# Moving loads to ScalarE's queue and making later weights earlier in a four-layer graph kernel

## The chip, the cores and the metric

The kernel runs on one core of a Trainium2 chip, in fp32. Time is the device time of one execution in microseconds (us). The executions of one kernel in one group differ by 0.2 to 0.8% from lowest to highest, so I give medians with the lowest and highest run. Verdicts use ratios: the mean time of one kernel's fast runs over the mean of the other's fast runs of the same rounds, so a ratio is not quite the quotient of the medians that I quote.

## The reference, cut to what matters

Four graph layers are applied in sequence to x of shape (8, 2048, 64), with one normalised 2048 x 2048 adjacency. Each begins with a layernorm and a relu and adds its result to x. Only layer 0 and the weights of the later layers matter here:

```python
# layer 0, in words: h = relu(layernorm(x)); T0 = h, T1 = A h, T2 = 2 A T1 - T0
# weights of a node n: sum over d of embedding[n, d] * weight[d, k]   (d = 16, k = 3)
# x += sum over k of T_k[n] @ W[n, k] + bias[n]
# layer 1: three steps, adjacency and an MLP with W1, W2, b1, b2
# layer 2: linear aggregation with w_nl, b_nl, then w_out, b_out
# layer 3: attention over the neighbours
```

## The kernel before

The eight batches are worked on as four pairs, p = 0 to 3, and the 2048 nodes as four blocks of 512, nb = 0 to 3. A product with the adjacency uses a high and a low half (H, L) of each operand. For pairs 2 and 3, T1 is made in layer 0 too (`term1`, the "first product"); the loop below then makes T2 (the "second product") and the node weights, block by block.

```python
    def load_h(p, nb, name, pool):            # h of one block, 256 KB, from memory
        t = pool.tile([P, 4, 2 * C], F32, tag="hb", name=f"hb_{name}", bufs=2)
        nc.sync.dma_start(t, hs[p][:, part(nb), :])
        return t

    def halves(src, name, pool=None):
        ...
        copies.append(nc.scalar.copy(Hq, src))                                        # "H" in traces
        nc.vector.tensor_tensor(Lq, src, Hq.bitcast(F32), op=ALU.subtract)   # "L" in traces
        return Hq, Lq

    def make_weights():
        ...                                   # small columns
        raw, tr, pr = (block("z", f"wz{i}", 3) for i in range(3))   # three tiles in all; norms use them too
        nc.gpsimd.memset(raw, 0.0)
        for i, w in enumerate((w1[:, :C], w1[:, C:], w2, w_out)):
            for hf in range(2):
                hs_ = slice(hf * C, (hf + 1) * C)
                nc.sync.dma_start(raw[hs_, i, hs_], w)
        nc.vector.tensor_copy(tr, transposed(lambda t: raw[:, t, :], "wT"))   # pt_wT on TensorE
        ...
        for i, (lhsT, rhs) in enumerate(pairs):
            nc.tensor.matmul(ps[:, i, :], lhsT, rhs, start=True, stop=True)   # wP
        nc.vector.tensor_copy(pr, ps)
        ...                                   # wb1s, rows of b_out and b2, scaling; then three stores to wD

    def node_weights(p, nb, terms, between=None):
        ...
                        nc.tensor.matmul(y[:, bb, :], terms[k][hs_, ts],
                            wt[hs_, k, dg * 512:(dg + 1) * 512], ...)         # y
        ...
                    last = nc.vector.scalar_tensor_tensor(                    # y pieces, "acc" and "odd"
                        xj, yd, ec, old, op0=ALU.mult, op1=ALU.add)

    for p in range(NP):
        def prepare(q):                       # halves of block q of the next pair
            if p == 0:
                src = l0q.tile([P, 512], F32, tag="hb", name=f"t1b_{nm}", bufs=2)
                nc.sync.dma_start(src, t1D[:, q * 512:(q + 1) * 512])
                hl_next.append(back(src, 1, q))
            elif p + 1 < NP:
                hl_next.append(halves(load_h(p + 1, q, nm, l0q), nm))
        ...
        for nb in range(NB):
            if p == NP - 1 and nb == 1:
                with tc.issue_after(chain[-1].ins):
                    make_weights()
            t2T = product(hl1, nb, nm, term(2, f"t2T_{nm}"), crow, ...)       # bv_0b to bv_3b
            ...
            t0T_next = feat_0(...)            # load_h, four transposes (pt), copy on ScalarE
            node_weights(p, nb, (t0T, t1T[nb], t2T), ...)
            t0T = t0T_next
            if nb in (1, 2):
                prepare(nb - 1)
```

Names in traces: bv_0a to bv_3a are the first product, bv_0b to bv_3b the second, pt the transposes of h, hb and hb_f loads of h, t1b loads of the second pair's T1, wz the three tiles of the weights. A program that builds the kernel puts the instructions of each engine in order; the source alone does not fix it.

## Time and profile before

| Quantity of the kernel before | value |
|---|---|
| median of 3 runs | 1300.35 us (1299.11 to 1302.89) |
| the unit of pair 3's block 1 (559.50 to 601.89 us) | 42.39 us |
| the unit after it | 28.90 us |
| half-clock stretch in the first of them | 13.65 us |
| gaps of TensorE over 1.3 us between 100 and 500 us, summed | 13.9 us |

The table is read so: TensorE sets the time, so a microsecond is won only where its stream has a gap or runs slowly. One unit has a slow stretch that its neighbour lacks; the gaps are elsewhere. A gap here is the time from the start of one matmul to the start of the next; the usual one is 0.23 us in a product and 0.43 us in a pair of y matmuls.

### The profile page before, as it was taken

How to read it: one execution, taken by the hardware profiler on the slowest of the kernel's cores; microseconds unless marked ns; L12 is line 12 of the kernel's file. 1: busy time of each engine (PE TensorE's matmuls, PEld its weight loads, DVE VectorE, ACT ScalarE, POOL GpSimd, SP SyncE). 2: the span in 40 equal slices, each digit the busy share in tenths (PEclk: the TensorE clock that was granted, in tenths of full speed). 3: DMA queues.
4: the chain of work that ended last, by engine and by line, in shares of the span. 5: the costliest groups of instructions: out<-in, count | busy, mean ns of one | idle time of the engine just before them, and what ended most of it. 6: DMA issues, size and time to landing. Idle time of an engine off the chain costs nothing.

```text
span 1295.8 us, 15644 instructions
## 1 busy us (share of the span) xinstructions
PE 1230.5 (95%) x5702; PEld 865.2 (67%) x5702; DVE 750.2 (58%) x1937; ACT 188.6 (15%) x313; POOL 224.6 (17%) x228
## 2 busy tenths in 40 slices
PE   3799999899999999999999999999999999989994
PEld 2476555455585556655558887878878878878883
DVE  5325887777747775357764435535644544566664
ACT  4541001000010000000011121112111211111110
POOL 4210111111121111011101024004201400332222
PEclk8799999999999999989999999999999999999997
DMA  9793334322343322123237535443653463433322
GB/s 252 227 240 114 86 94 111 93 73 63 95 104 82 81 78 68 35 55 86 58 83 174 107 90 158 115 93 106 159 118 90 139 130 94 151 102 106 97 67 52
DMA packets 149882, 140.11 MB, mean 108 GB/s; under 512 B 99892, under 2 KB 101940, under 8 KB 149796
## 3 DMA queue, kind: packets, MB, share of 16 engines
q1 hardware_dynamic: 137780, 106.54, 32.1%
q0 software_dynamic: 9904, 31.96, 8.7%
q8 instruction: 47, 0.77, 0.3%
q10 hardware_dynamic: 2112, 0.52, 0.2%
q14 instruction: 39, 0.32, 0.1%
HBM read 94.87 MB, written 35.73 MB: 101 GB/s over the span
## 4 chain that ended last, share of the span: by engine, by line
PE 77%; DMA 6%; DVE 6%; issue 6%; POOL 2%; ACT 1%; SPq 1%; ACTq 0%; POOLq 0%; DVEq 0%
PE bv L217 33%; PE y L580 22%; PE bn L523 4%; PE ph L742 3%; DMA st<-in_adj_dram 2%; PE bv_2b L217 2%; PE bv_3b L217 2%; DMA hb<-hs 2%; POOL rstd L169 1%; PE bv_1b L217 1%; PE bv_0a L217 1%; PE bn_u L523 1%; PE pt L229 1%; PE bv_0b L217 1%; DVE acc L589 1%
## 5 line engine op out<-in xcount | busy, mean ns | idle before, releaser
L217 PE MATMUL bv<-BT,H 128*128 128x512 f32 x1024 | 426.7, 417 | 0.0
L217 PE MATMUL bv<-BT,L 128*128 128x512 f32 x1024 | 401.3, 392 | 0.0
L217 PEld LDWEIGHTS bv<-BT,H 128*128 128x128 f32 x1024 | 192.9, 188 | 47.9 <-issue 11.5
L217 PEld LDWEIGHTS bv<-BT,L 128*128 128x128 f32 x1024 | 193.0, 188 | 47.5 <-issue 11.5
L589 DVE SCALAR_TENSOR_TENSOR acc<-y,emb,acc 128x128 f32<-128x128 f32 x512 | 176.3, 344 | 69.2 <-PE y L580 68.4
L580 PE MATMUL y<-wt,t0T 64*128 64x512 f32 x512 | 145.7, 611 | 9.2 <-DVE odd L589 9.2
L589 DVE SCALAR_TENSOR_TENSOR odd<-y,emb,odd 128x128 f32<-128x128 f32 x448 | 153.5, 343 | 0.0
L169 POOL TENSOR_TENSOR rstd<-var,mhalf 128x8 f32<-128x8 f32 x64 | 106.1, 1660 | 197.1 <-DVE var L167 191.6
L209 DVE TENSOR_TENSOR g<-bv,crow 128x512 f32<-128x512 f32 x48 | 33.2, 692 | 182.4 <-PE bv L217 182.4
L163 ACT ACTIVATE sq<-z 128x512 f32<-128x512 f32 x64 | 40.4, 631 | 404.9 <-DVE z L159 392.8
L580 PEld LDWEIGHTS y<-wt,t0T 64*128 64x128 f32 x512 | 46.8, 186 | 72.3 <-issue 66.5
L560 POOL TENSOR_TENSOR acc<-acc,wl 128x512 f32<-128x512 f32 x16 | 21.0, 1314 | 295.2 <-DVE z L159 294.0
L561 POOL DMA_DIRECT2D xs<-acc x32 | 18.0, 562 | 284.3 <-DVE acc L597 233.7
L580 PE MATMUL y<-wt,t1T 64*128 64x512 f32 x256 | 67.0, 589 | 0.0
L172 DVE SCALAR_TENSOR_TENSOR z<-z,rstd 128x512 f32<-128x512 f32 x64 | 44.7, 703 | 35.5 <-POOL rstd L169 35.5
L523 PEld LDWEIGHTS bn<-wl,g 128*128 128x128 f32 x384 | 49.4, 191 | 6.3 <-ACT g L747 3.1
L166 DVE TENSOR_REDUCE var<-sq 128x8 f32<-128x512 f32 x64 | 43.5, 680 | 16.1 <-ACT sq L163 16.1
L523 PE MATMUL bn<-wl,g 128*128 128x128 f32 x384 | 51.2, 276 | 0.7 <-ACT H L204 0.4
L689 DVE SCALAR_TENSOR_TENSOR junk<-mt,cols,st 128x512 uint8<-128x512 bf16 x64 | 49.2, 769 | 0.8 <-DMA mt<-MD 0.3
L580 PEld LDWEIGHTS y<-wt,t1T 64*128 64x128 f32 x256 | 27.6, 187 | 27.4 <-issue 27.1
L747 ACT ACTIVATE g<-g,b1s 128x512 f32<-128x512 f32 x32 | 23.2, 724 | 139.3 <-DVE g L746 139.3
L159 DVE TENSOR_TENSOR z<-acc,mean 128x512 f32<-128x512 f32 x56 | 38.3, 691 | 6.6 <-DMA hs<-z 5.0
(208 smaller groups left out, 1694.2 us busy)
## 6 DMA issues: line engine op xcount, KB each, us to landing
st<-in_adj_dram SPq DMA_DIRECT2D x128, 256.0 KB, 4.1
crow<-crowD SPq DMA_DIRECT2D x64, 256.0 KB, 3.3
hs<-z POOLq DMA_DIRECT2D x48, 256.0 KB, 2.9
hb<-hs SPq DMA_DIRECT2D x40, 256.0 KB, 3.3
xs<-acc POOLq DMA_DIRECT2D x32, 256.0 KB, 2.4
MD<-BT POOLq DMA_DIRECT2D x16, 512.0 KB, 5.1
acc<-xs SPq DMA_DIRECT2D x32, 256.0 KB, 3.5
acc<-in_x_dram SPq DMA_DIRECT2D x48, 128.0 KB, 3.7
```

Source lines behind the costliest of these rows:

```text
L159: nc.vector.tensor_tensor(g, groups(xt), mean[:, :, None].to_broadcast([P, 8, C]), op=ALU.subtract)
L163: nc.scalar.activation(sq, z, AF.Square)
L166: nc.vector.tensor_reduce(var, groups(sq), axis=AX.X, op=ALU.add)
L169: powers.append(nc.gpsimd.tensor_tensor(rstd, var, mhalf, op=ALU.pow))
L172: nc.vector.scalar_tensor_tensor(groups(h), g, 0.0, rstd[:, :, None].to_broadcast([P, 8, C]), op0=ALU.max, op1=ALU.mult)
L209: ahead.append(nc.vector.tensor_tensor(out, ps, crow, op=ALU.mult))
L217: nc.tensor.matmul(ps, hl[m // 4][i][:, m % 4, :], BT[:, m, nb * 512:(nb + 1) * 512], start=(m == 0 and i == 0), stop=(m == NCH - 1 and i ...
L523: nc.tensor.matmul(ps[:, t, :], fT[:, t * P:(t + 1) * P], wmat, start=True, stop=True)
L580: nc.tensor.matmul(y[:, bb, :], terms[k][hs_, ts], wt[hs_, k, dg * 512:(dg + 1) * 512], start=(k == 0), stop=(k == K - 1),)
L589: last = nc.vector.scalar_tensor_tensor(xj, yd, ec, old, op0=ALU.mult, op1=ALU.add)
L689: nc.vector.scalar_tensor_tensor(junk, mt, cols[:, i, :], st, op0=ALU.mult, op1=ALU.not_equal, accum_out=bad[:, i, q:q + 1],)
L742: fill[12] = lambda: nc.tensor.matmul(ph, w1v2 if s else w1vT, gT[nb], start=True, stop=True)
```

## The change

The intent is to take waits out of TensorE's stream. Part A splits the making of the weights into two stages, the source loads and all the rest, and moves both into the first product of pair 3, where no y work depends on VectorE's queue. Part B puts 32 loads (h, and T1 of the second pair) on ScalarE's queue, out of SyncE's.

```diff
     def load_h(p, nb, name, pool):
-        nc.sync.dma_start(t, hs[p][:, part(nb), :])
+        (nc.sync if lastp else nc.scalar).dma_start(t, hs[p][:, part(nb), :])
 ...                                          # the list lastp is made earlier
     def make_weights():
-        raw, tr, pr = (block("z", f"wz{i}", 3) for i in range(3))
+        raw = block("z", "wz0", 3)
         nc.gpsimd.memset(raw, 0.0)
         ...                                  # source loads
+        yield
+        tr, pr = (block("z", f"wz{i}", 3) for i in (1, 2))
         ...                                  # transposes, products, stores
+        yield
 ...
             if p == 0:
-                nc.sync.dma_start(src, t1D[:, q * 512:(q + 1) * 512])
+                nc.scalar.dma_start(src, t1D[:, q * 512:(q + 1) * 512])
 ...
         if p > 1:
-            t1T, hl1 = term1(p, hl, lambda nb: norm_0(p + 1, nb) if p + 1 < NP else None)
+            steps = make_weights()
+            def behind(nb):
+                if p + 1 < NP:
+                    norm_0(p + 1, nb)
+                elif nb in (0, 2):
+                    next(steps)
+            t1T, hl1 = term1(p, hl, behind)
         for nb in range(NB):
-            if p == NP - 1 and nb == 1:
-                with tc.issue_after(chain[-1].ins):
-                    make_weights()
```

More of the change, by code (lines that the diff above doesn't have):

```diff
@@ L197, in uniform_path @@
     copies = []
+    lastp = []
     def halves(src, name, pool=None):
@@ L506, in make_weights @@
         nc.gpsimd.dma_start(wD[:, 8:9], raw[:, 1:2, :])
-    lastp = []
+        yield
     w1e = consts.tile([P, P], F32, name="w1e")
```

## The prediction

> **What bounds the kernel now.** I read the page first, to see which engine and which wait carry the span, then the chain of work that ended last, then the busy time of each engine in single stages of layer 0, then the order of the built instructions before and after.
>
> From the page, busy time by engine and the chain's shares by engine:
>
> ```profile
> PE 1230.5 (95%) x5702; PEld 865.2 (67%) x5702; DVE 750.2 (58%) x1937; ACT 188.6 (15%) x313; POOL 224.6 (17%) x228
> ...
> PE 77%; DMA 6%; DVE 6%; issue 6%; POOL 2%; ACT 1%; SPq 1%; ACTq 0%; POOLq 0%; DVEq 0%
> ```
>
> TensorE (PE) is the bound: all the change can do is remove gaps in its stream or slow stretches of it, or add some. Layer 0 (about 105 to 670 us of the span) repeats one unit: a product of 32 matmuls (7.5 us) and 96 node-weight matmuls (21 us). I therefore compared one unit that contains the making of the later weights (pair 3, second block) with the next one that does not. The rows give the stretch, its length, busy us of PE, PEld, DVE, ACT and POOL with instructions, the granted clock, DMA share and GB/s:
>
> ```profile
> 559.50:601.89 42.39, 41.68 (x149) 20.76 (x147) 23.63 (x80) 1.52 (x3) 5.50 (x8) 0.84 0.25 68
> 601.89:630.79 28.90, 28.90 (x133) 16.04 (x133) 21.48 (x72) 1.22 (x2) 3.34 (x4) 1.00 0.28 64
> ```
>
> The unit with the weights takes 42.39 - 28.90 = 13.49 us longer, for only 16 more recorded matmuls, and its mean clock is 0.84. The chain in that unit (start, us, what) says why:
>
> ```profile
> 565.67 1.20 SPq L483
> ...
> 566.91 2.62 DMA wz<-in_L_gnn_W_dram
> 569.54 0.14 issue
> 569.67 0.30 PE pt_wT L229
> 569.98 1.05 PE y L580 x2
> ...
> 577.99 2.00 PE wP L490 x8
> 579.99 0.22 PE wb1s L493 x2
> 580.21 2.00 PE y L580 x2
> ...
> 601.89 7.49 PE bv_2b L217 x32
> ```
>
> The weight loads are issued at 565.67, just before TensorE reaches the transposes that need them (0.71 us idle). These sit singly between y matmuls, so y waits too; from 571.4 to 585.0 the recorded clock is 0.5, and two y matmuls take 2.00 us instead of 0.43. VectorE has long gaps here as well: 7.04 us before its first y piece, later 3.63 us before it copies wP, as that copy reuses a buffer still being stored.
>
> The other stalls of the stream in layer 0 come from loads of h. The same chain, around the first two blocks of pair 1:
>
> ```profile
> 237.00 0.51 SPq L126
> 237.62 4.08 DMA hb<-hs
> 241.72 0.63 ACT H L204
> ...
> 245.28 15.95 PE y L580 x72
> ...
> 268.71 0.45 PE pt L229 x4
> 269.18 3.44 DMA hb<-hs
> 272.64 0.63 ACT H L204
> ```
>
> VectorE takes its work in order: it waits for the H/L split of the loaded h, and TensorE then waits for VectorE to free y. Start-to-start times of the y matmuls give stalls above the usual 0.43 us of 3.6 us (245), 1.9 (276), 1.1 (395) and 2.1 (426). One more gap, about 1.8 us at 206, waits for an h load directly. That is about 10.5 us in all. What matters is what each load waited for: at 269.18, 388.76, 418.86 and 200.81 it was issued within 0.05 us after the transposes that read the buffer last; these are bound by the two buffers of "hb", not by SyncE. Only at 237.62 was the buffer free earlier (transposes done about 236.5) and SyncE was still issuing four loads of x.
>
> **What the Trainium skill says.** "TensorE: Matmul & The Clock Gate", section "What's actually happening": the array gets its half clock after an idle window of about 3.4 us and the full clock again after a busy one. The trace agrees: clock records are 0.5 or 1.0, and the slow one here lasts 13.65 us, four times 3.41. "DMA: Bandwidth & Descriptors", section "Issuing engines are not separate DMA queues": issuing on another engine only saves the sequencer's issue time, "usually small relative to the DMA itself". The trace agrees in size: an issue takes 0.32 to 0.9 us of SyncE, a 256 KB load of h 2.5 to 5.6 us to land. The same page, "Queues, rings and completion order": SyncE and ScalarE each own a queue on the same 16 engines, which take turns between queues; no run here shows yet what that does to h. "PSUM — Partial Sum Buffer", section "Engine vs sequencer instructions": the sequencer waits for earlier instructions only until they are dispatched. If that holds for loads on ScalarE, a load that stands behind a copy starts with that copy, not 0.6 us later. The trace before cannot show it: ScalarE's only loads are at the very start.
>
> **Part A: later weights in pair 3's first product.** The raw loads now stand on SyncE behind the first x load at about 505.4. Eight issues took 565.67 to 571.74, 6.1 us; so they are issued by about 512 and, at 2.0 to 3.3 us each, landed by 515. The transposes stand after the third block's product, at about 522: 7 us of slack, no wait. The transposes are four together and cost what pt_t costs, 0.44 us, with some 0.15 us for switching. Four product matmuls follow (0.9 us); wP then needs VectorE's copy of the transposes. VectorE does t1T first (522.2 to 522.9), and the 0.69 us copy ends near 524.0, when TensorE has been ready since 523.8: 0.2 us. The matmuls wP and wb1s took 2.22 us at half clock, so 1.1 us at full clock. Sum 0.44 + 0.15 + 0.2 + 1.1 = 1.9 us. The copy of wP no longer waits for the store of the first set, as the built order puts it before that set is scaled and gives it its own buffer. VectorE then waits for the broadcast of b_out (5.75 us to land before), to about 528.5, but next has to be ready only at about 530. The old unit becomes an ordinary one: -13.5 us. Net **-11.6 us**.
>
> **Part B: h and the second pair's T1 on ScalarE's queue.** 32 loads move, ScalarE's row goes from 641 to 673. ScalarE is 15% busy, so 32 issues of about 0.4 us (13 us, my estimate from SyncE's issue times) hide. By load that matters:
> - 237.62: issue becomes possible at 236.5 to 237.1; I take -1.0 us.
> - 269.18, 388.76, 418.86: still bound by the buffer. They stand behind the copy of t0T. If a load goes out as soon as the copy is dispatched, 0 to +0.1 each; no longer queued behind two x loads, perhaps -0.2 for two of them. I take -0.3 together.
> - 200.81: behind a copy too, and x loads can now interleave with it: +0.4.
> - 105.40: the first h load waits for the same memory to be free. The order puts its transposes two matmuls earlier on TensorE, which waits 2 x 0.23 us more: +0.4.
> - The scaling of w_nl moves to VectorE's row just ahead of the first t2T (114.83). Its loads landed at 115.6 before, but SyncE was stopped from about 109.2 to 109.8 by an h load and gave four h issues ahead of it; without those I estimate 113 to 114. No cost, little slack.
> Sum about **-0.5 us**, uncertain by 2.
>
> Total 1300.35 - 11.6 - 0.5 = 1288.3; I say 1288.5.
>
> **Rivals.**
> 1. A load on ScalarE starts only after the copy in front of it has finished. Then 0.6 us is added at 200, 269, 389 and 419 and the gain at 237 halves: Part B becomes about +3, the time 1292. For it: the built order does put the t0T copy ahead. Against it: the sentence on dispatch above.
> 2. The h loads were really late because of SyncE and of the x loads ahead of them on its queue. Then much of the 8.7 us of the four block stalls goes, and the time is 1283 to 1285. Against it: the load at 388.76 had no x load near it, landed in 2.72 us, and TensorE still lost 1.1 us.
> 3. The weight work only moves its cost: raw loads, b_out or the PSUM banks stall the new place, or the gaps bring the half clock again. A lost clock window costs half of 3.41, 1.7 us; with some 3 us of waits 1293. Against it: 7 us of slack and no TensorE gap expected above 0.3 us.
> 4. ScalarE, taking its queue in order, is blocked by a load that waits and delays squares and H copies. Only the loads behind H copies wait for VectorE, and ScalarE's next work is mostly 20 us later; little.
>
> **Range and chances.** Part A is read from two neighbouring units and firm to about 1.5 us; Part B from -4 to +3; the three runs before span 3.8 us. So 1284.5 to 1293. A gain over 2% needs 26 us: even all of A and every h stall come to about 24. Slower by over 2% needs a new stall of nearly 40 us.
>
> **What would show it.** The clock's record has no 0.5 stretch between 50 and 1130 us; the second block of pair 3 takes 28.9 us; the third to fourth block of its first product grows by about 1.9. The h load of pair 2's first block is issued about 1 us earlier after its transposes; the other three within 0.1 us as before (rival 1: 0.6 us later). After layer 0, everything is the same, shifted. I am wrong if the stalls at 276, 395 and 426 shrink to nothing, or if a new gap stands at 114, 206 or 524.

## The result, and the profile after

The changed kernel took 1289.32 us (1287.74 to 1292.68, 4 runs) against 1300.59 us (1299.11 to 1302.89, 4 runs) of before: ratio 0.9915, 95% interval 0.9891 to 0.994. That is an improvement by 0.8%, 0.8 us from the predicted 1288.5.

Busy time by engine and the chain's shares by engine, from the changed kernel's page:

```profile
PE 1224.0 (95%) x5702; PEld 864.7 (67%) x5702; DVE 750.9 (58%) x1937; ACT 188.6 (15%) x313; POOL 224.4 (17%) x228
...
PE 87%; DVE 5%; DMA 4%; POOL 2%; issue 2%; ACT 1%; SPq 0%; ACTq 0%; DVEq 0%; POOLq 0%
```

TensorE has the same number of instructions and 6.5 us less busy time: 12.8 us less in the unit that held the weights, against 4.8 us more between 105 and 506 us and 1.8 us more in the new place. Its share of the chain rose from 77% to 87%: the stretch in which the chain ran through the weights' loads is gone. The same two units as before (stretch, length, busy us of PE, PEld, DVE, ACT and POOL with instructions, granted clock, DMA share, GB/s):

```profile
567.96:596.87 28.91, 28.91 (x133) 16.04 (x133) 21.49 (x72) 1.51 (x3) 3.33 (x4) 1.00 0.29 69
596.87:625.76 28.89, 28.89 (x133) 16.05 (x133) 21.46 (x72) 1.22 (x2) 3.34 (x4) 1.00 0.27 64
```

The unit that held the weights is now like its neighbour: 13.48 us less, at full clock. What went to the new place is read from the chain there (start, us, what):

```profile
528.84 0.44 PE pt_t L230 x4
529.27 0.44 PE pt_wT L230 x4
529.71 0.93 PE bv_3a L218 x4
530.64 1.01 PE wP L494 x8
531.77 3.33 PE bv_3a L218 x14
...
567.96 7.48 PE bv_1b L218 x32
575.44 0.44 PE pt L230 x4
575.88 20.98 PE y L584 x96
```

Each piece follows the last without a gap: the transposes cost 0.44 us and the products 1.1 us, with four matmuls of bv_3a between them while VectorE copies. Against the trace of before, the distance by which this kernel lags grows from 6.64 us at the first matmul of this first product (506.30) to 8.39 us at that of bv_1b (567.89), so the new place costs 1.8 us. Part A is thus worth 13.48 - 1.8 = 11.7 us in the traces.

The stall at pair 2's first h load, which the prediction showed at 237.62, reads so after the change:

```profile
242.00 3.40 DMA hb<-hs
245.42 0.63 ACT H L205
...
248.98 15.95 PE y L584 x72
```

The load goes out at 242.00, right after the transposes that end at 241.89 and no longer behind loads of x, and TensorE's gap is 2.34 us instead of 4.07.

But the changed kernel lagged by 6.64 us before it came to the weights at all. In this execution Part B cost as much. Three half-clock windows of 3.41 us each (from 111.2, 210.2 and 281.9) lie in that part, where the trace of before has none; each costs at most half its length, 1.7 us. The profiled execution was also the slowest of the four. Whether the rest is the change or scatter had to be measured.

### The profile page after: what moved, and what is told of

Same layout as the page of the kernel before. It is cut to its first block, busy times and chain, and to the rows that moved or that the text cites. A ratio compares the mean times of both kernels' runs of the same rounds, so it can differ in the third digit from the quotient of the medians.

```text
span 1290.9 us, 15640 instructions
## 1 busy us (share of the span) xinstructions
PE 1224.0 (95%) x5702; PEld 864.7 (67%) x5702; DVE 750.9 (58%) x1937; ACT 188.6 (15%) x313; POOL 224.4 (17%) x228
## 4 chain that ended last, share of the span: by engine, by line
PE 87%; DVE 5%; DMA 4%; POOL 2%; issue 2%; ACT 1%; SPq 0%; ACTq 0%; DVEq 0%; POOLq 0%
PE bv L218 35%; PE y L584 24%; PE bn L527 4%; PE ph L751 3%; PE bv_2b L218 2%; PE bv_0b L218 2%; PE bv_3b L218 2%; PE bv_1b L218 2%; POOL rstd L169 1%; PE bv_0a L218 1%; PE bv_3a L218 1%; PE bv_2a L218 1%; PE pS L796 1%; PE bv_1a L218 1%; DMA hb<-hs 1%
## 5 line engine op out<-in xcount | busy, mean ns | idle before, releaser
L218 PEld LDWEIGHTS bv<-BT,H 128*128 128x128 f32 x1024 | 193.1, 189 | 48.0 <-issue 11.6
```

The source lines that it names most:

```text
L218: nc.tensor.matmul(ps, hl[m // 4][i][:, m % 4, :], BT[:, m, nb * 512:(nb + 1) * 512], start=(m == 0 and i == 0), stop=(m == NCH - 1 and i ...
```

## The experiments

Twelve runs followed, the changed kernel once more and eleven others, all correct, each timed in five rounds beside the kernel before on the same chip. They came in four groups. The table gives the median, the ratio to before with its interval, and the sum of TensorE's gaps over 1.3 us between 100 and 500 us in the profiled execution (worked out from the starts of the matmuls).

| run | group | median us | ratio, 95% | gaps us |
|---|---|---|---|---|
| after_again | 1 | 1285.65 | 0.9896, 0.9882 to 0.991 | 15.4 |
| a_alone | 1 | 1286.41 | 0.991, 0.9897 to 0.9923 | 13.1 |
| b_alone | 1 | 1301.22 | 1.0027, 1.0013 to 1.004 | 16.4 |
| early_old | 1 | 1297.41 | 0.9997, 0.9982 to 1.0011 | 16.6 |
| early_old_zt | 2 | 1290.41 | 0.9928, 0.9904 to 0.9952 | 16.3 |
| t2one | 2 | 1301.97 | 1.0013, 0.9994 to 1.0033 | 26.4 |
| hb3 | 2 | 1288.53 | 0.9914, 0.9892 to 0.9936 | 13.1 |
| a_hb3 | 2 | 1281.12 | 0.9856, 0.9833 to 0.9879 | 8.1 |
| p0sync | 3 | 1288.38 | 0.991, 0.9895 to 0.9925 | 12.8 |
| a_alone_lp | 3 | 1280.78 | 0.9853, 0.9835 to 0.9872 | 3.4 |
| a_hb3_lp | 3 | 1278.19 | 0.9827, 0.981 to 0.9844 | 2.7 |
| before_zt | 4 | 1294.38 | 0.9965, 0.995 to 0.998 | 12.5 |

In the first trace of the changed kernel this sum was 16.0 us. The kernel before had medians of 1298.67, 1299.9, 1299.54 and 1299.82 us in the four groups, from 11, 11, 11 and 16 runs.

### after_again: the change once more

No edit.

> The changed kernel again beside the others on the same chip, for the differences of parts and for a second profile: about 1289. If the three 3.4 us stretches of half clock in the first profile (at 111, 210 and 282 us) are an accident[...], this profile has another number of them or other places; if they follow from the change, they are all there again.

It measured 1285.65 us (1283.14 to 1289.35), ratio 0.9896. Its trace has one half-clock window of 3.41 us before 500 us instead of three, and that one at another place: from 428.5, after the gap at 427. None of the three came back at its place, so where they fall is scatter between executions, and a single profile of this kernel must not be read to 2 us.

### a_alone: the weights early, all loads on SyncE

```diff
-        (nc.sync if lastp else nc.scalar).dma_start(t, hs[p][:, part(nb), :])
+        nc.sync.dma_start(t, hs[p][:, part(nb), :])
-                nc.scalar.dma_start(src, t1D[:, q * 512:(q + 1) * 512])
+                nc.sync.dma_start(src, t1D[:, q * 512:(q + 1) * 512])
```

> Part A alone: weights in two stages as in the changed kernel, all loads of h and of the second pair's T1 back on SyncE. My theory (Part A is the whole gain, Part B about nothing): 1300.6 - 11.6 = about 1289, within 1.5 us of the changed kernel; in the profile the second block of pair 3 takes 28.9 us, the stalls of layer 0 in front of the h loads stay as in the kernel before, and the first load of h lands after about 3.7 us, not 4.9. Rival (Part B helps once the queue is free): 2 us or more slower than the changed kernel. Second rival (Part B costs what the profile of the changed kernel shows, about 5 us): 1285 to 1287.

0.991 is a gain of 0.9%, 1298.67 x 0.009 = 11.7 us (10.0 to 13.4 by the interval), which is what the traces gave for Part A. Part A alone carries the whole gain. The bare 1286.41 us lies in the range of the second rival too; but before and the changed kernel were faster too in this group (1298.67 and 1285.65), and the rival asked for the changed kernel to be some 5 us slower than a_alone.

### b_alone: the loads on ScalarE, the weights where they were

```diff
-        nc.sync.dma_start(t, hs[p][:, part(nb), :])
+        (nc.sync if lastp else nc.scalar).dma_start(t, hs[p][:, part(nb), :])
-                nc.sync.dma_start(src, t1D[:, q * 512:(q + 1) * 512])
+                nc.scalar.dma_start(src, t1D[:, q * 512:(q + 1) * 512])
```

> Part B alone: loads on ScalarE's queue, weights at the old place. My theory: 1299.5 to 1302, no gain; the unit with the weights still takes about 42.4 us with the recorded clock at 0.5 for about 13.7 us. Rival (Part B helps): 1297 or less. Second rival (costs 5 us): 1305 to 1306.

The time is as expected, and so is the unit with the weights: 42.2 us, with 13.65 us at half clock. The kernel is slower than before by 0.27%, some 3.5 us, with an interval clear of 1. Yet on top of Part A the same edit cost nothing in time (after_again against a_alone, intervals overlapping). The two pairs of traces agree better. TensorE's gaps at the same six places (us from start to start; "none" is below 0.8):

| place | waits for | before | b_alone | a_alone | after_again |
|---|---|---|---|---|---|
| near 110 | first h load | none | 2.32 | none | 2.17 |
| near 207 | h, pair 1 | 2.14 | 2.28 | 2.16 | 2.31 |
| near 245 | h, pair 2 | 4.07 | 2.30 | 4.26 | 2.43 |
| near 276 | h, pair 2 | 2.29 | 3.50 | 1.80 | 2.43 |
| near 395 | h, pair 3 | 1.57 | 1.50 | 1.43 | 1.50 |
| near 426 | h, pair 3 | 2.50 | 3.21 | 2.14 | 3.20 |

One gap shrinks by 1.8 us, one of about 2.2 us is new, the one near 276 grows by 1.2 and 0.6 us, and the last by 0.7 and 1.1 us. The sums of all gaps in the table above rise by 2.5 us (13.9 to 16.4) and by 2.3 us (13.1 to 15.4). All traces with two tiles for the loads and the usual order agree: 15.4 to 16.6 us in the five with the whole of Part B, 12.5 to 13.9 us in the three without it (before, a_alone, before_zt). So Part B works where it was meant to, at 245, and loses the gain elsewhere.

The new gap is the wait for the first load of h. In the chain of a_alone:

```profile
103.97 3.68 DMA hb_f<-hs
...
107.69 0.66 PE pt L230 x4
```

and of b_alone:

```profile
104.86 4.87 DMA hb_f<-hs
...
109.77 0.66 PE pt L230 x4
```

The load in front of 276 takes longer as well: 3.5 to 4.7 us in the same five traces, 2.95 to 3.44 us in the three without Part B.

### early_old: the source loads early, the rest in its old unit

From the changed kernel, the second stage goes back to pair 3's block 1:

```diff
-                elif nb in (0, 2):
+                elif nb == 0:
                     next(steps)
 ...
         for nb in range(NB):
+            if p == NP - 1 and nb == 1:
+                with tc.issue_after(chain[-1].ins):
+                    next(steps)
```

> As the changed kernel, but only the first stage (the raw loads) stands in pair 3's first product; transposes and products stand again at the second block of its second product. Theory that the late loads caused the slow stretch: nearly all of Part A stays, within 1 us of the changed kernel, the transposes wait for nothing and the clock stays 1.0 there. Rival, that the place among the node weights is what costs (VectorE's in-order copies between y pieces): 4 us or more are lost again, the unit takes over 33 us.

My theory was that the late source loads made the old unit slow. It missed: 0.9997, nothing gained, which is the number that the rival had, although the loads had landed by 518.8 us and the transposes ran at 564.3 us without waiting. Three lines of the trace in that unit (start, us, engine, line, operation, tile; idle time before it and what ended it) tell why:

```profile
574.72 0.55 POOL L508 DMA_DIRECT2D wD<-wz  x1
...
581.25 0.69 DVE L495 COPY wz<-wP 128x512 f32<-128x512 f32 x1 [6.53 <-DMA wD<-wz]
...
584.48 1.22 PE L584 MATMUL y<-wt,t0T 64*128 64x512 f32 x2 [5.30 <-DVE odd L593]
```

VectorE copies the products into the third tile of the weights. With the source tile held since the first product, and norms using the same three tiles, the third tile got the room of the second. Its copy must wait until GpSimd's store of the second tile has landed: issued at 574.72, landed at 581.16. VectorE works in order, so the y pieces behind the copy wait 6.53 us as well. TensorE runs out of free y banks and stands for 5.30 us, and the clock is at half for 6.83 us. The wait for loads was gone, and a wait for room stood in its place.

The kernel before had that wait too, behind the loads, as this line of its own trace shows:

```profile
584.49 0.69 DVE L491 COPY wz<-wP 128x512 f32<-128x512 f32 x1 [3.63 <-DMA wD<-wz]
```

### early_old_zt and before_zt: the same with room of its own

In each, the third tile gets its own room, and one t2 tile instead of two pays for it. From early_old and from before (there the first line makes `raw` as well):

```diff
-        tr, pr = (block("z", f"wz{i}", 3) for i in (1, 2))
+        tr, pr = block("z", "wz1", 3), l0q.tile([P, 4, 2 * C], F32, name="wzp")
-        return pool.tile([P, 512], F32, tag=f"t{k}", name=name, bufs=(2, 4, 2)[k])
+        return pool.tile([P, 512], F32, tag=f"t{k}", name=name, bufs=(2, 4, 1)[k])
```

> early_old again (the changed kernel with the second stage of the weights left in the unit of pair 3's second block, its source loads early), but the third tile of the weights, the one that receives the products, no longer comes from the three tiles of tag z: it has its own room, which is made by one t2 tile in place of two. In the trace of early_old the products' copy on VectorE waited 6.53 us for a store of the weights (issued 574.72, landed 581.16) because it was to use the same room as the tile being stored; all y pieces behind it on VectorE waited too, and the clock fell to half for 6.83 us. Theory (late source loads made the old unit long, and in early_old the wait for the tile's room took their place at the same spot): the unit of pair 3's block 1 falls from over 40 us to 30 to 32 us, and the time is that of the changed kernel, 0.988 to 0.992 of before, 11 to 16 us under it. Rival (the work has no cheap place inside the second product, whatever it waits for): 0.997 to 1.001, as early_old.

> The kernel before, with the source loads of the weights as late as they were, but the tile that receives the products has its own room (one t2 tile in place of two; the built order of TensorE differs in two neighbouring matmuls only). It completes a square: late loads and shared room (before), early loads and shared room (early_old, 0.9997), early loads and own room (early_old_zt, 0.9928), late loads and own room (this). Theory (the late loads alone start the slow stretch, as the clock fell to half at 571.4, nine microseconds before VectorE began its wait for the room at 580.9; the room's wait only prolongs it by 3.63 us at most): 1 to 4 us less than before, 0.997 to 0.999, with a half-clock stretch of 10 us or more and a unit of pair 3's block 1 of 38 to 41 us. Rival (the room is the whole cause): 0.990 to 0.993, and a unit of 30 to 32 us. Second rival (either cause alone gives the whole loss): 1.000, and 42 us.

The unit in early_old_zt, from the chain of waits:

```profile
561.81 0.59 PE pt_wT L230 x4
562.40 5.48 PE bv_1b L218 x24
567.88 0.89 PE wP L494 x8
...
568.89 1.95 PE bv_1b L218 x8
570.84 0.44 PE pt L230 x4
571.28 20.98 PE y L584 x96
592.26 7.46 PE bv_2b L218 x32
```

The same work in the same place now costs next to nothing: no gap, no half clock. In before_zt, with the loads late, the chain still starts at a load of the weights:

```profile
569.80 2.48 DMA wz<-in_L_gnn_W_dram
...
572.42 0.30 PE pt_wT L229
572.72 1.05 PE y L580 x2
...
576.12 2.00 PE y L580 x2
...
580.54 2.00 PE wP L490 x8
```

The four kernels make a square; each entry is the time between the first recorded matmuls of bv_1b and bv_2b, and the half-clock stretch in it (with early loads the weights' transposes, 0.44 to 0.59 us, stand just ahead of the unit and are not in it):

| | shared room | own room |
|---|---|---|
| source loads late | before: 42.3 us, 13.65 us | before_zt: 39.6 us, 10.24 us |
| source loads early | early_old: 38.5 us, 6.83 us | early_old_zt: 30.0 us, none |

Taking away one cause alone wins 3.8 or 2.8 us (from times before rounding); taking away both wins 12.3 us. With either one alone a half-clock stretch remains. "Early" changes more than the loads, though: the built order then puts the four transposes together ahead of the unit and wP into its product, where with late loads both stand among the y matmuls. The runs do not separate the lateness of the loads from this order.

Nor is the half clock the whole of the slow stretch. Its 13.65 us cost at most half, 6.8 us, of the 13.5 us that the unit lost. In the kernel before, the y matmuls among the transposes start one by one, every 0.53 us before the clock falls (569.90, 570.44) and every 1.01 us after it (580.14, 581.15). In early_old they start in pairs, every 0.43 us at full and every 0.85 us at half clock. The prediction's "2.00 us instead of 0.43" is thus both effects together. Why the pairs broke up is not shown.

The time of before_zt (0.9965, 4.5 us less by the ratio, expected 1 to 4) falls at the edge of the theory and outside both rivals. That of early_old_zt (0.9928, 9.4 us less than before; expected 11 to 16) is a little short of the theory's and well outside the rival's; it contains Part B, as early_old does, and its runs spread widely (1285.54 to 1295.47).

So the first theory fell in its simple form. The late loads, with the order that goes with them, began the slow stretch, but the room would have kept most of it. The change won because its place removes both: in the first product the copy of wP comes before the second tile's scaling and store, with room of its own.

### t2one: a control that was none

```diff
-        return pool.tile([P, 512], F32, tag=f"t{k}", name=name, bufs=(2, 4, 2)[k])
+        return pool.tile([P, 512], F32, tag=f"t{k}", name=name, bufs=(2, 4, 1)[k])
```

> Control: the changed kernel with one t2 tile in place of two, nothing else. TensorE works through the units in order, so the next t2 tile is written when the matmuls that read the last one are long over. Expected: as the changed kernel, within 0.1% of it (0.988 to 0.991 of before). If it is slower, the three other runs of this group must be read against it.

It was slower than the changed kernel by about 1%. The built order shows why: with one t2 tile the y matmuls of pair 0's first block moved behind most of the product of its third, and the others followed. New gaps of 5.25 us (ending at 164) and 6.88 us (at 197) opened in the trace. I had reasoned about a wait and overlooked that the order itself may change. The other kernels with one t2 tile were compared before they ran: TensorE's order in early_old_zt, hb3 and a_hb3 is the same, instruction by instruction, as in early_old, after and a_alone, and in before_zt it differs from before by two neighbouring matmuls. So the t2 tile does not disturb them by its order; a clean measure of the tile alone I don't have.

### hb3 and a_hb3: a third tile for the loads

From the changed kernel, and the same with both loads on SyncE's queue:

```diff
-        t = pool.tile([P, 4, 2 * C], F32, tag="hb", name=f"hb_{name}", bufs=2)
+        t = pool.tile([P, 4, 2 * C], F32, tag="hb", name=f"hb_{name}", bufs=2 if lastp else 3)
-                src = l0q.tile([P, 512], F32, tag="hb", name=f"t1b_{nm}", bufs=2)
+                src = l0q.tile([P, 512], F32, tag="hb", name=f"t1b_{nm}", bufs=3)
                                               # and one t2 tile, as above
```

> The changed kernel with three tiles for the loads of h and of the second pair's T1 in place of two (and one t2 tile). Theory: what these loads wait for is that one of the two tiles comes free, which is when TensorE's transposes have read it; the queue that issues them matters little. Then the five gaps of 1.5 to 3.2 us at which TensorE waits for such a load between 200 and 430 us (together about 11.9 us in the repeat of the changed kernel, about 10 above the usual spacing) shrink to below 0.5 us each: 6 to 10 us less than the changed kernel, 0.982 to 0.985 of before. Rival (place in ScalarE's queue): the loads stay behind the copies of the block before, and no more than 0 to 3 us are won. The first gap, at 110 us, has no earlier tile to wait for and stays under both.

> The same three tiles, with both loads back on SyncE's queue (weights early, as in the changed kernel). Theory of the tiles: the gaps shrink here too, 6 to 10 us less than a_alone, 0.983 to 0.986 of before, and within 3 us of hb3. Rival (ScalarE's queue is what lets the loads go early): SyncE's queue holds them behind loads that wait for other tiles, the gaps stay at 1.4 to 4.3 us, and the time stays at a_alone's 0.991.

On SyncE the theory held for the time: a_hb3 is at 0.9856, 7 us under a_alone (0.991 - 0.9856, of 1299), though three gaps stayed (216, 247 and 393). On ScalarE it missed: hb3 stays at the changed kernel's time, so a_hb3 is not within 3 us of it, as I had expected. The gap near 207 is gone there, but a worse one opened just after it (chain of hb3):

```profile
208.10 5.62 DMA hb<-hs
...
213.75 0.63 ACT H L205
...
214.40 0.03 DVE L L206
...
217.31 18.23 PE y L584 x72
```

With three tiles, the load of pair 2's first block goes out at 208.10, right behind another h load on ScalarE at 207.68, and takes 5.62 us. But the build has put its low half (L) a unit earlier in VectorE's row, so VectorE stands before it, with the y pieces behind. In a_hb3 the same low half is early too, with a gap of 3.16 us at 216. That suggested another cause than the queue or the number of tiles: VectorE, in order, waits for a low half that nothing needs until pair 2's first product begins, at about 350 us. The next two kernels test it.

### a_alone_lp and a_hb3_lp: the low halves on GpSimd

```diff
-    def halves(src, name, pool=None):
+    def halves(src, name, pool=None, sub=None):
-        nc.vector.tensor_tensor(Lq, src, Hq.bitcast(F32), op=ALU.subtract)
+        (sub or nc.vector).tensor_tensor(Lq, src, Hq.bitcast(F32), op=ALU.subtract)
-                hl_next.append(halves(load_h(p + 1, q, nm, l0q), nm))
+                hl_next.append(halves(load_h(p + 1, q, nm, l0q), nm, sub=nc.gpsimd))
```

> a_alone (weights early, loads on SyncE's queue, two tiles) with the low halves of pairs 2 and 3, eight subtractions of 128x512, made by GpSimd instead of VectorE. In the trace of a_alone four gaps of TensorE at 244, 276, 395 and 425 us (4.26, 1.80, 1.43 and 2.14 us, 9.6 in all, about 8.6 above the usual spacing) end with a chain load of h, copy on ScalarE, low half on VectorE, then the y pieces that stand behind the low half in VectorE's queue. Theory (the wait is VectorE's, in order, for a value that nothing needs yet): the four gaps go, 6 to 9 us less than a_alone, 0.984 to 0.987 of before. Rival (the load is what binds: the copy or GpSimd's own queue passes the wait on, through the reciprocal root that the norms need): 0 to 2 us.

> a_hb3 (three tiles for the loads, on SyncE's queue) with the same eight subtractions on GpSimd. In a_hb3 the gaps before the transposes of the second and third pair went, but three were left behind the low half on VectorE, at 216, 247 and 393 us (3.16, 2.25, 1.37 us, 6.8 in all). Theory: they go, 4 to 6 us less than a_hb3, 0.981 to 0.983 of before. Rival: as a_hb3, 0.985 to 0.987.

In a_alone, one of the four gaps reads so in the chain:

```profile
236.22 4.24 DMA hb<-hs
...
240.48 0.63 ACT H L205
...
241.13 0.04 DVE L L206
...
244.04 17.50 PE y L584 x72
```

In a_alone_lp all four gaps are gone, and the eight subtractions stand in GpSimd's row (operation, tile, shapes, count; busy us and mean ns; idle before them and what ended it):

```profile
L206 POOL TENSOR_TENSOR L<-hb,H 128x512 fp32r<-128x512 f32 x8 | 10.7, 1342 | 32.3 <-ACT H L205 32.3
```

Each takes twice as long as on VectorE (1.34 us against 0.69), and GpSimd stands 32.3 us waiting for them, but TensorE does not notice. The time is 0.9853, 7.4 us under a_alone by the ratios, 5.6 by the medians (expected 6 to 9); the two intervals are clear of each other. With three tiles as well, a_hb3_lp is at 0.9827, 3.8 us under a_hb3 (expected 4 to 6; one gap of 1.42 us is left at 248). These two intervals overlap, and so does that of a_alone_lp, so this last step is not clear of noise. By its median it is the fastest kernel: 1278.19 us (1275.74 to 1279.75, 5 runs), under both the kernel before and the changed one.

### p0sync: the first pair's loads back on SyncE

```diff
-        (nc.sync if lastp else nc.scalar).dma_start(t, hs[p][:, part(nb), :])
+        (nc.sync if lastp or p == 0 else nc.scalar).dma_start(t, hs[p][:, part(nb), :])
```

> The changed kernel with the four loads of h of pair 0 back on SyncE's queue; the other loads stay on ScalarE's. Theory (what the change of queue loses lies at the first load of the layer, which took 3.65 to 3.68 us on SyncE's queue and 4.72 to 4.91 us on ScalarE's, was followed by a second gap of 2.0 to 2.4 us that the kernels with SyncE's queue don't have, and the five later waits only trade tenths of a microsecond): 2 to 4 us less than the changed kernel, 0.987 to 0.989 of before, and the gap before the second transpose near 110 us is gone. Rival (the loss is spread over the later loads, or comes from the second pair's T1): as the changed kernel, 0.990 to 0.991.

The trace did what was expected: the first load took 4.02 us instead of 4.72, and the second gap near 110 us fell to 0.99 us. The time did not: 0.991 is what the rival had, and cannot be told from after_again's 0.9896. Effects of 2 us are at the limit of what five rounds separate. What Part B is worth in time therefore stays open between about nothing and a loss of 3.5 us.

## Why the prediction was right

**The bound.** TensorE was the bound and stayed it. This held in every run.

**Part A, -11.6 us.** It was -11.7 us in the traces, and 0.991 with Part A alone. Its terms held: the old unit gave 13.48 us (13.5 predicted), the new place cost 1.8 us (1.9). The source loads had landed by 520.7, 8.5 us before the transposes (7 predicted). The copy of wP waits for no room in the new place, as the step on the built order said. The prediction named the late loads and mentioned the room in passing; the square shows that in the old place early loads alone would have won only a third of the unit's excess. The prediction also said that the trace agrees with a half clock that follows an idle window of about 3.4 us. The record shows 0.5 and 1.0 and lengths that are multiples of 3.41 us, but not the idle window: in the 3.41 us before 571.37 the longest gap was 1.30 us from start to start. And it set "2.00 us instead of 0.43" beside the half clock, which accounts for 0.85 of the 2.00.

**Part B, -0.5 us, uncertain by 2.** The sign of the sum was probably wrong. By its terms, b_alone against before and after_again against a_alone: the load at 237 was to win 1.0 us and won 1.8; the first load was to lose 0.4 us and opened a gap of about 2.2 us, because it took 4.72 to 4.91 us on ScalarE's queue where it took 3.65 to 3.68 us on SyncE's; the load near 200 was to lose 0.4 and lost 0.15; the three others were to win 0.3 together and lost 1.9 and 1.8 us. In place of -0.5 the gaps say +2.3 to +2.5, which the range from -4 to +3 contained. Two terms are mis-sized, for the same reason: I counted from when a load is issued, and left out that the load itself would be slower. That holds at the first load and at 276; at 426 the load went out 0.4 us after the transposes, and how long it took was not recorded. That the total came within 0.8 us of the median is therefore partly luck: with +2.4 in place of -0.5 the same sum gives 1291.2. The four runs themselves differ by 4.9 us.

**Rivals.** The first (a load on ScalarE starts after the copy in front of it) fell: the loads go out about 0.1 us after the transposes in three cases and 0.4 us in one. The second (SyncE made the loads late) fell as a whole with b_alone, which wins nothing; at 245 alone it was so. The third (the weights only move their cost) did not come true in the new place, but early_old shows it in another: there the cost did move, into the wait for room. The fourth (ScalarE blocked) is not seen; the blocked engine is VectorE.

**What would show it.** One sign was wrong: I had said that no half-clock stretch would lie between 50 and 1130 us. There were three of one window, in the repeat one. One follows the new gap near 110 us, two follow gaps that the old kernel had as well, where they may or may not come. No new gap stood at 114 or at 524; one stood near 110.

## What to carry to other kernels

When work makes a neighbouring engine stall, count every wait in the stretch, not the first: here late loads and a shared tile each kept the slow stretch alive, one of the two removed won a third or less of what the unit had lost, and both together won nearly all. Before another queue is tried for a late load, look who stands behind its consumer: the eight subtractions that held up VectorE's row cost 7 us, and moving them to an engine with room won what moving the loads could not. And compare the built order before calling a kernel a control; one tile fewer cost 1% through the order alone.

## What the Trainium skill lacked or had wrong

- "TensorE: Matmul & The Clock Gate", section "HAM oscillation — how this bites in real kernels", gives as abstract rule that gaps over about 3.4 us are to be avoided. In the first trace of the changed kernel a gap of 2.30 us from start to start (ending at 210.09) was followed at 210.2 by a half-clock window of 3.41 us, and likewise one of 2.89 us (at 280.5, window from 281.9). The repeat had 2.31 and 2.43 us at these places and no such window. In the kernel before, b_alone and before_zt the clock fell (at 571.37, 572.73 and 574.32) with no gap over 1.30 us in the 3.41 us ahead of it. So shorter gaps can cost a window too, and not in every execution. The page's next section does let frequent short idle times upset the clock, but gives no length for them.
- "DMA: Bandwidth & Descriptors", section "Issuing engines are not separate DMA queues", says that the choice of issuing engine only saves issue time. The runs agree that it wins little, but it can also lose: the first h load landed 3.65 to 4.05 us after its issue in the five traces that have it on SyncE's queue (before, a_alone, a_alone_lp, before_zt, and p0sync with 4.02) and 4.50 to 5.03 us in the seven that have it on ScalarE's (4.72 in after_again, 4.91 in after, 4.87 in b_alone).
- "PSUM — Partial Sum Buffer", section "Engine vs sequencer instructions", has semaphore operations as its example. The traces show the same for the issue of a load on ScalarE: in hb3 a load is issued at 203.16 while the copy before it runs from 203.07 to 203.66. The page's strict order of VectorE's queue is what the low halves show: 7.4 us were won when they left it.
